# Second layer's first slabs loaded through the last feed-forward part, their differences tied behind it; projections' first weights and one chain placed anew

## The chip, the cores and the metric

The kernel runs on one core of one Trainium2 chip. The metric is device time in microseconds (us): the median of three runs for the kernel as it was, and one further execution that the hardware profiler recorded. All data is float32. The engines are named as in the profile: PE (TensorE; PEld is its weight load), DVE (VectorE), ACT (ScalarE), POOL (GpSimd) and SP (SyncE, which here only issues DMAs).

## The reference

Two layers are computed one after the other on `x` of shape (B, T, F, H) = (4, 512, 128, 64), that is D = F*H = 8192 channels for each of 512 time steps.

```python
# layer 0, per batch b
xn = layernorm(x.reshape(b, t, d), ...)
k, v, r = xn @ Wk, xn @ Wv, sigmoid(xn @ Wr)          # (8192 -> 64 each)
states = scan(s -> decay * s + k * v, over t)
x = x + (r * states @ Wo)                             # 64 -> 8192
xn = layernorm(x);  x = x + gelu(conv over f, 3 taps, 64 -> 64 channels)
xn = layernorm(x);  to = causal conv over t, 3 taps, each channel by itself
x = x + layernorm(to)
x = x + (gelu(x @ W1 + b1) @ W2 + b2)                 # per f: 64 -> 256 -> 64
# layer 1
trend = moving average of x over t, 25 wide
xf = rfft(x - trend, axis=1)[:, :128]                 # 128 modes
ys = einsum('bmnc,cmk->bknc', xf, w_real + 1j * w_imag)
return trend + irfft(ys, n=512)
```

## The kernel before

**Layer 0** (`layer0`, L80) works with channels on the partitions: 8192 channels are 32 pairs (NPR = 32) of 128-channel chunks, each pair a tile of 128 x 2 x 512. For each batch it runs stages: `project` J (loads `xt`, multiplies with the weights `wx`), `scan` Z, `attend_and_convolve` A, `convolve_time` C, `open_feed` O and `feed_forward` F. Each is a Python generator that yields a share of its work; `in_turn` (L835) draws from two of them at a time, so that, for instance, the feed-forward of batch 2 lies between the pieces of the time convolution of batch 3. A generator that yields CHAIN hands over at a place where a chain of small operations runs. The order of matmuls on PE is exactly the order in which the generators are drawn (a manual schedule for that engine). The other engines' instructions are ordered by a planner, by priority; `tc.keep_in_program_order` pins one to its place in the program, and `tc.issue_after(ins)` asks that what is issued inside it comes after `ins`.

The stages draw buffers from pools: `fr` (tiles `xp`, `x1`, `z` and, as a fourth kind, `wx`), `bk` (fetched and intermediate tiles, `kx`, `kh`, `kd`, `k3`, `mid`, `sq`), `const` and others. The last pair of stages is the feed-forward of batch 3 with nothing beside it.

What the change touches in layer 0:

- *The end of a sum over channels.* `add_up` (L252) lets PE add the channels of each tile and its squares into a PSUM bank. `finish` (L256) has ACT copy the bank to `s_sb` (L260) and, after a CHAIN yield, has PE turn it (L264) and DVE copy the means (L269). `moments` (L272) then makes the variance (L275, L276 on DVE), the reciprocal root (L233, L234 on POOL) and the product `mrs` (L278 on DVE). `rows` (L280) spreads each over the partitions (L242 on PE) and copies it out (L286 on ACT), with a CHAIN yield after each. The time convolution ends with `finish` and `moments`; `open_feed`, which begins with `rows`, follows.
- *The first weights of a projection.* For batches 2 and 3, `project` loads weights for the first two pairs (L351), and `scale_weights` (L358) multiplies them in place on DVE, pinned to program order. The matmuls of the projection are at L408. Before it in the same turn lies the end of `attend_and_convolve` of the previous batch, whose last DVE work for a pair is the sum `x2` (L568), stored by POOL (L569).
- *The feed-forward.* Pair i needs the residual: `fetch` (L607) has SP load `kx` and `kh`, DVE computes L692, L693, ACT L701, DVE the sum `x3` (L704). `widen` (L725) is four quarters of eight PE matmuls (L733) with a gelu on ACT each (L738); `narrow` (L740) multiplies back (L746 on PE into `p` and `pb`), and DVE adds the residual (L759) into `x4s`, which for these batches lies in `wx` tiles. `store` (L762), two pairs later, transposes on PE (L765), ACT copies out of PSUM (L773, L778), and POOL stores `ob` to the array `x4` in DRAM (L774).

**Layer 1** (`layer1`, L880) reads `x4` from DRAM. Each batch has 16 slabs of 512 columns. `transform` (L943) goes through them in groups of two; two batches are transformed, then mixed. `shifted_slab` (L934) has SP load one slab with three DMAs (L938, L939, L940; 1.05 MB together) into `xin`, one of five buffers `big` of the pool `io`. ACT copies some edge rows (L956), once for the first and twice for the second slab of a group; DVE makes the difference `v` (L959), the sum `u` (L960) and from that `ev` (L963, two half-size operations a slab). PE multiplies `v` (L971), `ev` (L979) and the edges (L988) with the transform matrices, and ACT copies the banks to `xf` (L995). The inverse tables are loaded by DMAs on ACT's queue (L901). `mix` (L997) and `invert` (L1027) follow. The five buffers are shared by the slabs of the transform, the weights of `mix` and the slabs of `invert`.

Pools are laid out one after the other, and a pool of layer 1 takes the addresses of pools of layer 0 that were given back. The `io` pool thus lies where `fr`, with its `wx` tiles, lay: the first write to it waits for the last reads of what was there.

Of the kernel before, what the change touches and what calls it, by code (L numbers as in the profile page):

```python
# [1 line left out]

# [1 line left out]

# [41 lines left out]
@with_exitstack  # L46
def conv_seq_kernel(
    ctx: ExitStack,
    tc: tile.TileContext,
    x: bass.AP,  # L50
    xt: bass.AP,
    vecs: bass.AP,
    wkvr: bass.AP,
    wo: bass.AP,
    wdec: bass.AP,
    wconv: bass.AP,
    fbias: bass.AP,
    w1: bass.AP,
    fb1: bass.AP,
    w2: bass.AP,  # L60
    fb2: bass.AP,
    wri: bass.AP,
    dftv: bass.AP,
    dftd: bass.AP,
    dfte: bass.AP,
    idfte: bass.AP,
    idfto: bass.AP,
    avg: bass.AP,
    avgh: bass.AP,
    out: bass.AP,  # L70
):
    B = x.shape[0]
    dram = ctx.enter_context(tc.tile_pool(name="dram", bufs=1, space=DRAM))
    x4 = [dram.tile([T, D], F32, tag=f"x4_{b}", name=f"x4_{b}") for b in range(B)]

    layer0(tc, dram, x, xt, vecs, wkvr, wo, wdec, wconv, fbias, w1, fb1, w2, fb2, x4)
    layer1(tc, x4, wri, dftv, dftd, dfte, idfte, idfto, avg, avgh, out)


@with_exitstack  # L80
def layer0(ctx, tc, dram, x, xt, vecs, wkvr, wo, wdec, wconv, fbias, w1, fb1, w2, fb2, x4):
# [10 lines left out]

    decay = ctx.enter_context(tc.tile_pool(name="decay", bufs=1))
    fr = ctx.enter_context(tc.tile_pool(name="fr", bufs=3))
    const = ctx.enter_context(tc.tile_pool(name="const", bufs=1))
    bk = ctx.enter_context(tc.tile_pool(name="bk", bufs=2))
    rowp = ctx.enter_context(tc.tile_pool(name="rowp", bufs=1))
# [49 lines left out]
    nc.vector.tensor_copy(decb, dec.to_broadcast([P, T]))  # L147


    cgr = const.tile([P, NPR, H], F32, name="cgr")  # L150

    at_one = const.tile([P, 2], F32, name="at_one")
    nc.vector.tensor_reduce(at_one[:, 0:1], ident.rearrange("p (q k) -> p q k", k=32)[:, :, 1], mybir.AxisListType.X, ALU.add)
# [142 lines left out]
        return xp  # L296

    def spare(tag, n):
        return fr.tile([P, 2, n], F32, tag=tag, name=tag, bufs={"z": 4, "wx": 2}.get(tag, 3))

    def c_bank():
        return two(ps_c, "c")
# [17 lines left out]
    held = [False]  # L320
    narrowly = set()
    unscanned = [True]


    def project(b):
# [36 lines left out]
        ws, xps, xks = {}, {}, {}  # L362
        if b > 1:
            weights(0)
            for k in range(2):
                scale_weights(k, ws[k], True)
            xps[0] = load_x(b, 0)
        for i in range(NPR):
            first, last = i == 0, i == NPR - 1
# [146 lines left out]
    def attend_and_convolve(b):  # L516
# [29 lines left out]
        def convolve(i):  # L546
            cv = c_bank() if i % 2 or held[0] else two(ps_m, "m")
            for h in range(2):
                for j in range(2):
                    q = 32 * (2 * h + j)  # L550
                    nc.tensor.matmul(
                        cv[h * H : (h + 1) * H, j, :], lhsT=cgr[q : q + 2, i, :], rhs=mb[q : q + 2, :],
                        start=True, stop=False,
                    )
            for j in range(2):
                c = 2 * i + j
                for n, h in neighbours(i % 2, c):
                    if 0 <= n < NCH:
                        rs = halves[rows_of(n // 2 % 2, n - c)]
                        nc.tensor.matmul(  # L560
                            cv[halves[h], j, :], lhsT=ws[n][rs, P:], rhs=zs[n][rs, :], start=False, stop=False
                        )
            for j in range(2):
                c = 2 * i + j
                nc.tensor.matmul(cv[:, j, :], lhsT=ws[c][:, 0:P], rhs=zs[c], start=False, stop=True)
            nc.scalar.activation(cv, cv, AF.Gelu_apprx_tanh)
            x2 = two(bk, "x2")
            nc.vector.tensor_tensor(x2, cv, x1s.pop(i), ALU.add)  # L568
            nc.gpsimd.dma_start(x2d[b][2 * i : 2 * i + 2].rearrange("c p t -> p c t"), x2)  # L569
            sq2 = bk.tile([P, 2, SL], F32, tag="sq", name="sq2")  # L570
            nc.scalar.activation(sq2, x2, AF.Square)  # L571
            for c in (2 * i - 2, 2 * i - 1):
                zs.pop(c, None)
                ws.pop(c, None)
            if i + 2 < NPR:
                scaled(i + 2)
            waiting[i] = x2, sq2
# [26 lines left out]

    def fetch(tag, src, b, i):
        t = bk.tile([P, 2, SL], F32, tag=tag, name=tag, bufs=3 if tag == "kx" else 2)
        nc.sync.dma_start(t, src[b][2 * i : 2 * i + 2].rearrange("c p t -> p c t"))  # L607
        return t


# [36 lines left out]
    def convolve_time(b):  # L647
# [34 lines left out]
            yield 7.0 * (NPR + 2) / (n + 2)  # L682
        mean, sq = yield from finish(st, bank, 4)
        causal[b] = moments(mean, sq, 4)


    def residual(b, i):
# [27 lines left out]
    def feed_forward(b):  # L715
# [12 lines left out]
        def widen(i, q):  # L728
            x3 = x3s[i]
            pm = unit()  # L730
            for h in range(2):
                for j in range(2):
                    nc.tensor.matmul(  # L733
                        pm[halves[j], h, :], lhsT=w1_sb[halves[h], q * H : (q + 1) * H], rhs=x3[halves[h], j, :],
                        start=True, stop=True,
                    )
            mid = mids[i, q] = bk.tile([P, 2, SL], F32, tag="mid", name="mid", bufs=4)
            nc.scalar.activation(mid, pm, AF.Gelu_apprx_tanh, bias=fb1_sb[:, q : q + 1])  # L738

        def narrow(i, q):  # L740
            if q == 0:
                sums2[i] = of_p(), ps_s.tile([P, SL], F32, tag="s", name="pb")
            mid = mids.pop((i, q))
            for h in range(2):
                for j in range(2):
                    nc.tensor.matmul(  # L746
                        sums2[i][j][halves[h], :], lhsT=w2_sb[halves[j], q, :], rhs=mid[halves[j], h, :],
                        start=q == 0, stop=q == 3,
                    )
            if q < 3:  # L750
                return
            x3 = x3s.pop(i)
            if lag > 1:
                pair = spare("wx", 4 * S + SL)[:, :, 0:SL]
                x4s[i] = [pair[:, j, :] for j in range(2)]
            else:
                x4s[i] = [bk.tile([P, SL], F32, tag="x4t", name="x4t", bufs=3) for _ in range(2)]
            for j, pa in enumerate(sums2.pop(i)):
                nc.vector.scalar_tensor_tensor(x4s[i][j], pa, fb2_sb, x3[:, j, :], ALU.add, ALU.add)  # L759

        def store(i):
            pt = unit()  # L762
# [22 lines left out]
        for i in range(NPR + lag):  # L785
            if i >= lag:
                store(i - lag)
            for q in range(4):
                done += quarter
                if i < NPR:  # L790
                    if q < 2:
                        widen(i, q + 2)
                    elif i + 1 < NPR:
                        widen(i + 1, q - 2)
                    if i + 2 < NPR and q == 1:
                        coming = residual(b, i + 2)
                    if i + 2 < NPR and q == 3:
                        x3s[i + 2] = add_residual(b, i + 2, *coming)
                    narrow(i, q)
# [62 lines left out]
    with tc.manual_schedule(engines={nc.tensor.engine}):  # L862
        for _ in project(0):
# [10 lines left out]
            ((2, (O, 0.05), (F, 0.95)), (3, (C, 0.95), (O, 0.05))),  # L874
            ((3, (F, 1.0)), (3, (nothing, 1.0))),
        )


@with_exitstack
def layer1(ctx, tc, x4, wri, dftv, dftd, dfte, idfte, idfto, avg, avgh, out):  # L880

# [7 lines left out]
    G = 2  # L891

    dft = ctx.enter_context(tc.tile_pool(name="dft", bufs=1))
    io = ctx.enter_context(tc.tile_pool(name="io", bufs=2))
    const = ctx.enter_context(tc.tile_pool(name="const1", bufs=1))
    spec = ctx.enter_context(tc.tile_pool(name="spec", bufs=1))
# [29 lines left out]
            nc.vector.tensor_copy(dst, src)  # L926

    def slab(b, s):
        xin = io.tile([P, NT, SL], F32, tag="big", name="xin", bufs=5)
        nc.sync.dma_start(  # L930
            xin, x4[b][:, s * SL : (s + 1) * SL].rearrange("(c p) d -> p c d", p=P)
        )
        return xin

    def shifted_slab(b, s):
        xin = io.tile([P, NT, SL], F32, tag="big", name="xin", bufs=5)
        c = slice(s * SL, (s + 1) * SL)
        nc.sync.dma_start(xin[TURN:P, 0, :], x4[b][0 : P - TURN, c])  # L938
        nc.sync.dma_start(xin[0:TURN, 0, :], x4[b][T - TURN : T, c])  # L939
        nc.sync.dma_start(xin[:, 1:NT, :], x4[b][P - TURN : T - TURN, c].rearrange("(c p) d -> p c d", p=P))  # L940
        return xin

    def transform(b, xf):  # L943

        for g in range(NS // 2):
            edge = io.tile([P, SL], F32, tag="edge", name="edge")
            uv, ev, pf = [], [], []
            for k in range(2):
                s = 2 * g + k
                c = slice(s * SL, (s + 1) * SL)  # L950
                xin = shifted_slab(b, s)
                ends = xin[0 : 2 * TURN, 0, :]
                if k == 0:
                    first = ends
                for q in (32,) if k == 0 else (H, H + 32):
                    nc.scalar.copy(edge[q : q + 2 * TURN, :], ends)  # L956
                u = io.tile([P, 2, SL], F32, tag="uv0", name="u")
                v = io.tile([P, 2, SL], F32, tag="uv1", name="v")
                nc.vector.tensor_tensor(v, xin[:, 0:2, :], xin[:, 2:4, :], ALU.subtract)  # L959
                nc.vector.tensor_tensor(u, xin[:, 0:2, :], xin[:, 2:4, :], ALU.add)  # L960
                t = io.tile([P, 2, SL], F32, tag="ev", name="ev")
                for i, op in enumerate((ALU.add, ALU.subtract)):
# [34 lines left out]
    def mix(xf):  # L997

        xc = xf.rearrange("p b r (a c l) -> p b r a c l", c=H, l=2)
        for g in range(H // CG):  # L1000

            w = io.tile([P, CG, 2, 2, M], F32, tag="big", name="w", bufs=5)
            nc.sync.dma_start(w, wri[:, g * CG : (g + 1) * CG, :, :, :])
            w4 = w[:, :, 1, 0, :].rearrange("p c (n i m) -> p c n i m", n=2, i=2)[:, :, :, 0, :]
            for t in (w4, w[:, :, 1, 1, 0:H]):
# [23 lines left out]
    def invert(b, xf):  # L1029
# [3 lines left out]
        def waves(s):  # L1033
# [12 lines left out]
            for i, op in enumerate((ALU.add, ALU.subtract)):  # L1046
                nc.vector.tensor_tensor(even[:, i, :], ev[0], two, op)
            for i in range(2):
                pm = io.tile([P, 2, SL], F32, tag=f"uv{i}", name="pm")
                for k, op in enumerate((ALU.add, ALU.subtract)):  # L1050
                    nc.vector.tensor_tensor(pm[:, k, :], even[:, i, :], od[i], op)
                halves[s].append(pm)
# [1 line left out]
        def trends(s):  # L1054
            c = slice(s * SL, (s + 1) * SL)
            xin = slab(b, s)
            halo = io.tile([P, SL], F32, tag="edge", name="halo")
            for j in range(NT):
                at = 32 * j
                if j > 0:  # L1060
# [137 lines left out]
```

## Time and profile before

| what | us |
|---|---|
| median of three runs | 3730.86 |
| lowest and highest | 3727.31, 3736.47 |
| the profiled execution's own time | 3727.17 |
| its span, first to last instruction | 3725.4 |
| PE busy | 3519.4 |
| DVE busy | 2671.6 |
| ACT busy | 1779.8 |
| POOL busy | 450.4 |
| granted PE clock, mean share of full | 0.983 |

A row of the groups or the timeline gives line, engine and operation, then output and input tiles with their shapes. In the timeline the first number is the start from the span's begin, the second the duration, and the bracket at the end how long the engine had stood idle and what released it. A row of the list of waits gives who waited for whom, the total, how often, and the longest. Matmuls overlap in PE's pipeline, and their ends are modelled; a busy PE is not a PE at its peak.

### The profile page before, as it was taken

Reading aid. Unit: us, or ns where it says so; the run is one execution under the profiler, and the core shown is the slowest. Engines: PE = TensorE matmul, PEld = TensorE weight load, DVE = VectorE, ACT = ScalarE, POOL = GpSimd, SP = SyncE. Lnnn points to the kernel's source line nnn. Section 1 sums busy time; section 2 is a strip of 40 time slices with the busy share of each in tenths; the row PEclk is TensorE's granted clock in tenths of the full one; section 3 lists DMA queues with packets and bytes.
Section 4 is the critical chain, followed back from the end, with each engine's and each line's share of the span. In section 5 each row is a group of like instructions: output and inputs, shape, how many; then the busy total and the mean of one; then the engine's idle time right before and its main releaser. Section 6 shows DMA issues by size and latency. Waiting matters only on the chain. (4 is left out here: it accounts for less than half of the span.)

```text
span 3725.4 us, 53006 instructions
## 1 busy us (share of the span) xinstructions
PE 3519.4 (94%) x20041; PEld 1366.8 (37%) x20041; DVE 2671.6 (72%) x3498; ACT 1779.8 (48%) x2331; POOL 450.4 (12%) x654
## 2 busy tenths in 40 slices
PE   9999999989999999999999989899989999899998
PEld 4433322224333223433322333333323843328433
DVE  4455569976777896677789699946658277792677
ACT  0013346546666565566656588878855200152100
POOL 0000012220011211001122122100000000001000
PEclk9999999999999999999999999999999999999999
DMA  9867647777885787788478677645569479994687
GB/s 313 282 211 243 227 154 270 254 264 259 293 295 176 249 275 267 265 292 296 167 240 286 210 245 268 233 154 194 199 202 285 154 231 295 300 295 167 214 286 263
DMA packets 427223, 910.29 MB, mean 244 GB/s; under 512 B 32728, under 2 KB 83160, under 8 KB 422872
## 3 DMA queue, kind: packets, MB, share of 16 engines
q1 hardware_dynamic: 353136, 636.92, 52.7%
q0 software_dynamic: 71680, 268.46, 19.8%
q8 instruction: 160, 2.62, 0.3%
q10 hardware_dynamic: 2152, 1.51, 0.1%
q14 instruction: 95, 0.78, 0.1%
HBM read 638.26 MB, written 268.50 MB: 243 GB/s over the span
## 5 line engine op out<-in xcount | busy, mean ns | idle before, releaser
L746 PE MATMUL p<-mid,w_sb 64*64 64x512 f32 x2048 | 560.8, 595 | 24.0 <-DVE wx L759 23.3
L746 PE MATMUL pb<-mid,w_sb 64*64 64x512 f32 x2048 | 533.4, 595 | 0.0
L738 ACT ACTIVATE mid<-c,fb_sb 128x1024 f32<-128x1024 f32 x256 | 284.6, 1112 | 94.5 <-PE c L733 92.3
L738 ACT ACTIVATE mid<-m,fb_sb 128x1024 f32<-128x1024 f32 x256 | 285.0, 1113 | 91.2 <-PE m L733 89.7
L733 PE MATMUL c<-x,w_sb 64*64 64x512 f32 x2016 | 281.6, 606 | 11.1 <-ACT mid L738 7.0
L733 PE MATMUL m<-x,w_sb 64*64 64x512 f32 x2016 | 283.3, 609 | 5.6 <-ACT ob L778 3.4
L746 PEld LDWEIGHTS p<-mid,w_sb 64*64 64x64 f32 x2048 | 160.4, 134 | 289.6 <-issue 244.0
L408 PE MATMUL a<-xp,wx 128*128 128x512 f32 x512 | 240.0, 613 | 6.6 <-issue 6.6
L1044 ACT COPY two<-a 128x512 f32<-128x512 f32 x64 | 37.5, 587 | 428.4 <-PE a L1039 428.4
L1067 PE MATMUL b<-xin,avg_sb 128*128 128x512 f32 x512 | 230.8, 593 | 3.3 <-DVE xin L1073 3.3
L1073 DVE TENSOR_TENSOR xin<-b,pm 128x512 f32<-128x512 f32 x256 | 159.1, 684 | 99.2 <-PE b L1070 84.3
L571 ACT ACTIVATE sq<-x 128x1024 f32<-128x1024 f32 x128 | 135.2, 1056 | 181.4 <-DVE x L568 181.3
L626 DVE SCALAR_TENSOR_TENSOR to<-kd,vec,to 128x510 f32<-128x510 f32 (+1 forms) x272 | 197.7, 747 | 10.5 <-ACT to L622 9.4
L701 ACT ACTIVATE kd<-kd,vec 128x512 f32<-128x512 f32 x256 | 193.1, 805 | 3.3 <-DVE kd L693 3.3
L252 PE MATMUL st<-x,ones 128*32 128x512 f32 x512 | 174.2, 611 | 10.7 <-DVE x L568 10.6
L926 DVE COPY xf<-b 128x256 f32<-128x256 f32 x128 | 54.4, 425 | 178.9 <-PE b L1013 170.0
L626 DVE SCALAR_TENSOR_TENSOR z<-x,vec,z 128x511 f32<-128x511 f32 x240 | 176.2, 747 | 5.0 <-ACT z L622 3.6
L704 DVE TENSOR_TENSOR x<-kd,kx 128x1024 f32<-128x1024 f32 x126 | 154.2, 1224 | 33.8 <-ACT kd L701 33.8
L532 DVE TENSOR_TENSOR x<-a,xp 128x1024 f32<-128x1024 f32 x128 | 156.3, 1221 | 29.8 <-PE a L530 27.3
L530 PE MATMUL a<-rst,wo_sb 64*128 64x512 f32 x512 | 148.6, 654 | 27.4 <-DVE x L532 25.4
L759 DVE SCALAR_TENSOR_TENSOR x4t<-p,fb_sb,x 128x512 f32<-128x512 f32 x64 | 47.8, 747 | 159.8 <-PE pb L746 157.4
L569 POOL DMA_DIRECT2D x<-x x128 | 93.5, 731 | 566.7 <-DVE x L568 561.7
(269 smaller groups left out, 6830.1 us busy)
## 6 DMA issues: line engine op xcount, KB each, us to landing
xp<-in_xt SPq DMA_DIRECT2D x256, 512.0 KB
kh<-to SPq DMA_DIRECT2D x156, 512.0 KB
x<-x POOLq DMA_DIRECT2D x128, 512.0 KB, 4.6
kx<-x SPq DMA_DIRECT2D x128, 512.0 KB
x<-ob POOLq DMA_DIRECT2D x64, 1024.0 KB, 8.1
xin<-x SPq DMA_DIRECT2D x64, 1024.0 KB
out<-xin POOLq DMA_DIRECT2D x64, 1024.0 KB, 5.9
x<-x SPq DMA_DIRECT2D x96, 512.0 KB
```

The lines of the kernel that those rows point to most:

```text
L252: nc.tensor.matmul(st[32 * q : 32 * q + 32, :], lhsT=ones, rhs=src[:, j, :], start=first, stop=last,)
L408: nc.tensor.matmul(pa[:, k, :], lhsT=wq[:, j, k * P : (k + 1) * P], rhs=xp[:, j, :], start=first and j == 0, stop=last and j == 1,)
L530: nc.tensor.matmul(at[:, j, :], lhsT=wo_sb[js, :], rhs=rst[js, :], start=True, stop=True)
L532: nc.vector.tensor_tensor(x1, at, xp, ALU.add)
L626: tap = nc.vector.scalar_tensor_tensor(to[:, j, k:], xr[:, j, : SL - k], vec[:, w, c], to[:, j, k:], ALU.mult, ALU.add)
L701: tc.keep_in_program_order(nc.scalar.activation(d[:, j, :], d[:, j, :], AF.Identity, bias=vec[:, B4, c], scale=vec[:, G4, c]))
L704: nc.vector.tensor_tensor(x3, d, x2, ALU.add)
L733: nc.tensor.matmul(pm[halves[j], h, :], lhsT=w1_sb[halves[h], q * H : (q + 1) * H], rhs=x3[halves[h], j, :], start=True, stop=True,)
L738: nc.scalar.activation(mid, pm, AF.Gelu_apprx_tanh, bias=fb1_sb[:, q : q + 1])
L746: nc.tensor.matmul(sums2[i][j][halves[h], :], lhsT=w2_sb[halves[j], q, :], rhs=mid[halves[j], h, :], start=q == 0, stop=q == 3,)
L1067: nc.tensor.matmul(po[j], lhsT=avg_sb[:, j, :], rhs=xin[:, j, :], start=True, stop=False)
L1073: nc.vector.tensor_tensor(by_n(xin[:, j, :]), by_n(po[j]), by_c(pm[j % 2][:, j // 2, :]), ALU.add)
```

## The change

It has four parts. First, layer 1 gets a pool `slabs` of its own for the five `big` buffers, the edge rows and the differences `v`, placed ahead of `io`, where layer 0's `decay` and `fr` lay; layer 0 moves `wx` out of `fr` into a new pool `wxp`, and the tile `cgr` from `const` into `fr`. Second, the loads of slabs 0 to 4 of batch 0 are issued after fetches of the feed-forward of batch 3 (pairs 12, 16, 20, 24 and 28 are then being fetched), their edge copies after the last gelu of pair 29, and the first two `v` after the last residual sum of pair 29. Third, the time convolution of batch 3 yields CHAIN once more at its end, after `moments`. Fourth, for batches 2 and 3 the first weights' scalings are no longer pinned in program order but tied behind the sum `x2` of pair 30 of the batch before.

In the order that results, PE's instructions differ in one place alone: between L264 of the time convolution of batch 3 and its first spread L242 there now stand the transposes of one pair and three units of the feed-forward of batch 2 (L733 and L746), and three fewer stand after it. On SP the fifteen slab DMAs stand between the fetches, three after every fourth pair. On ACT five edge copies stand between two gelus of pairs 29 and 30, and the sixth one gelu later. On DVE two `v` stand before the residual sums of pair 30, and the scalings stand before the last L568 of the batch before. POOL's order is the same.

```diff
@@ layer0
     fr = ctx.enter_context(tc.tile_pool(name="fr", bufs=3))
+    wxp = ctx.enter_context(tc.tile_pool(name="wxp", bufs=2))
...
-    cgr = const.tile([P, NPR, H], F32, name="cgr")
+    cgr = fr.tile([P, NPR, H], F32, name="cgr", bufs=1)
...
     def spare(tag, n):
-        return fr.tile([P, 2, n], F32, tag=tag, name=tag, bufs={"z": 4, "wx": 2}.get(tag, 3))
+        if tag == "wx":
+            return wxp.tile([P, 2, n], F32, tag=tag, name=tag)
+        return fr.tile([P, 2, n], F32, tag=tag, name=tag, bufs=4 if tag == "z" else 3)
...
+    last_fetch = [None]
+    after = {"sync": []}
@@ project
         if b > 1:
             weights(0)
-            for k in range(2):
-                scale_weights(k, ws[k], True)
+            with tc.issue_after(begin[project]):
+                for k in range(2):
+                    scale_weights(k, ws[k])
@@ attend_and_convolve
-            nc.vector.tensor_tensor(x2, cv, x1s.pop(i), ALU.add)
+            whole_x2 = nc.vector.tensor_tensor(x2, cv, x1s.pop(i), ALU.add)
+            if i == NPR - 2:
+                begin[project] = whole_x2.ins
@@ fetch
-        nc.sync.dma_start(t, src[b][2 * i : 2 * i + 2].rearrange("c p t -> p c t"))
+        last_fetch[0] = nc.sync.dma_start(t, src[b][2 * i : 2 * i + 2].rearrange("c p t -> p c t"))
@@ convolve_time
         causal[b] = moments(mean, sq, 4)
+        if b == B - 1:
+            yield CHAIN
@@ feed_forward, widen
+            gelu = nc.scalar.activation(mid, pm, AF.Gelu_apprx_tanh, bias=fb1_sb[:, q : q + 1])
+            if i == NPR - 3:
+                after["scalar"] = gelu.ins
@@ feed_forward, narrow
+                summed = nc.vector.scalar_tensor_tensor(x4s[i][j], pa, fb2_sb, x3[:, j, :], ALU.add, ALU.add)
+            if i == NPR - 3:
+                after["vector"] = summed.ins
@@ feed_forward
                         coming = residual(b, i + 2)
+                        if b == B - 1 and i % 4 == 2:
+                            after["sync"].append(last_fetch[0].ins)
@@ layer1
+    slabs = ctx.enter_context(tc.tile_pool(name="slabs", bufs=2))
     io = ctx.enter_context(tc.tile_pool(name="io", bufs=2))
...
+    def behind(b, s, ins):
+        return tc.issue_after(ins) if b == 0 and s < 5 else nullcontext()
@@ transform
-                xin = shifted_slab(b, s)
+                with behind(b, s, after["sync"][min(s, 4) + 2]):
+                    xin = shifted_slab(b, s)
...
-                    nc.scalar.copy(edge[q : q + 2 * TURN, :], ends)
+                with behind(b, s, after["scalar"]):
+                    for q in (32,) if k == 0 else (H, H + 32):
+                        nc.scalar.copy(edge[q : q + 2 * TURN, :], ends)
...
-                v = io.tile([P, 2, SL], F32, tag="uv1", name="v")
-                nc.vector.tensor_tensor(v, xin[:, 0:2, :], xin[:, 2:4, :], ALU.subtract)
+                v = slabs.tile([P, 2, SL], F32, tag="uv1", name="v")
+                with behind(b, s, after["vector"]):
+                    nc.vector.tensor_tensor(v, xin[:, 0:2, :], xin[:, 2:4, :], ALU.subtract)
```

## The prediction

> **What bounds the kernel now.** I read the page first: engines, then the costliest groups. The first line says that TensorE (PE) is the bound nearly throughout.
>
> ```profile
> PE 3519.4 (94%) x20041; PEld 1366.8 (37%) x20041; DVE 2671.6 (72%) x3498; ACT 1779.8 (48%) x2331; POOL 450.4 (12%) x654
> ```
>
> The change takes no matmul away, so it can win only among the 3725.4 - 3519.4 = 206 us in which PE stands. PE's list of waits says whose they are (total, count, longest):
>
> ```profile
> PE a L971 <- DVE v L959: 20.4, 12, 9.4
> PE a L242 <- POOL rs L234: 12.3, 6, 4.0
> PE a L408 <- issue: 6.6, 2, 4.1
> ```
>
> Row one is the second layer's transform, waiting for the slabs' differences `v`. Row two holds the wait for the moments' reciprocal root, row three the projections of batches 2 and 3 (two waits in all). The timelines of PE, DVE, SP and ACT around these places then give the sizes. The largest, between the layers (start, duration, engine, line, what, idle before):
>
> ```profile
> 2742.55 1.31 PE L765 MATMUL c<-ident,wx 128*128 128x128 f32 x8
> 2753.26 3.37 PE L971 MATMUL a<-v,dftd_sb 128*64 128x512 f32 x8 [9.40 <-DVE v L959]
> 2758.30 1.94 PE L971 MATMUL a<-v,dftd_sb 128*64 128x512 f32 x8 [1.68 <-DVE v L959]
> ```
>
> ```profile
> 2744.01 0.34 SPq L938 DMA_DIRECT2D xin<-x  x1
> ```
>
> ```profile
> 2751.93 1.22 DVE L959 TENSOR_TENSOR v<-xin 128x1024 f32<-128x1024 f32 x1 [8.78 <-DMA xin<-x]
> 2834.25 2.50 DVE L963 TENSOR_TENSOR ev<-u 128x512 f32<-128x512 f32 x4
> 2841.20 2.50 DVE L963 TENSOR_TENSOR ev<-u 128x512 f32<-128x512 f32 x4
> ```
>
> PE's last transposes (L765) end at 2743.86, only then does SP issue slab 0 (2744.01), it lands at 2751.9, and PE starts at 2753.26. Later a group of two slabs takes 6.95 us (from 2834.25 to 2841.20), which is DVE's work: two `v` and two `u` of 1.13 each, four half-size `ev`, 2.4. PE needs 3.65 + 1.9 + 1.1 = 6.65. So late in the transform DVE is the bound and PE waits 0.4 a group.
>
> **Part 1: slabs 0 to 4 early.** *Removed*: the release wait and the landing of slab 0. *Added to the feed-forward of batch 3 (2482 to 2744)*: 15 DMAs on SP, three a slab, one slab per four pairs behind a fetch of L607; six edge copies on ACT; two `v` on DVE.
>
> The DMAs: 1.05 MB a slab beside a stage whose window from 2500 to 2700 us shows DMA engines 0.56 busy. At the 3.5 us a slab of the late transform this is 17.5 us of transfer in 262 us. The slab stands in SP's queue ahead of the next pair's fetches and can delay them by its 3.5. Their lead covers it: the last `kh` is issued at 2698.95 and first read by L692 at 2714.00, 15 us later. Without this cover each slab would cost up to 3.5. I take 0 (ends 0 and 5 in all). POOL's stores are untouched.
>
> The edge copies are not free. They sit on ACT behind a gelu (L738) of pair 29, ahead of the next gelu:
>
> ```profile
> 2723.06 1.11 ACT L738 ACTIVATE mid<-c,fb_sb 128x1024 f32<-128x1024 f32 x1 [0.25 <-PE c L733]
> 2724.78 1.11 ACT L738 ACTIVATE mid<-m,fb_sb 128x1024 f32<-128x1024 f32 x1 [0.60 <-PE m L733]
> ```
>
> ACT idles 0.6 per 1.72 us unit there. Five copies of 0.635 (three took 1.90 at 2757.46) are 3.2; less the 0.6, a gelu, and the narrowing matmuls that need it, come 2.5 late. PE is full, so I book 2.4 (ends 1 and 4): its end goes to 2746.3. The two `v` fit in DVE's idle of 5 us a pair: nothing.
>
> Then PE needs only the last PSUM copy (L773), at about 2747.4. DVE does sixteen groups of 6.95 less the two `v`: 111.2 - 2.3 = 108.9 from 2746.3, so to 2855.2; PE's tail behind the last `ev` is 3.1 (before: 2872.7 to 2875.8). That is 2858.3 against 2875.8. Slab 5 can't be issued before group 0's edge matmuls have read slab 0's buffer (2747.4 + 6.65 = 2754) and lands some 7 later, while DVE wants it at about 2759: 2 to 4 us of stall. End 2861.5: **gain 14.3**.
>
> Two rates speak for less. The Trainium skill's page "DMA: Bandwidth & Descriptors", section Specifications, gives a core about 358 GB/s from HBM: 27 slabs of 1.05 MB would take 79 us, no bound at all. The rows say otherwise: in the window 2820 to 2840 the engines moved 293 GB/s at 0.97 busy, so 27 slabs cost 97 us of the 104 from 2754 to the end. I use the row: DMA barely keeps up, and at 3.7 us a slab (the early spacing, 2769.01 to 2772.70) the end is 2754 + 7 + 26 x 3.7 + 6.5 = 2864: gain 12. Low end 8 (ACT: its loads of the inverse tables, L901, wait for the last store to land, issued about 2748 in the new kernel, and the `xf` copies that free PSUM queue behind them; wanted at 2761, margin 1 to 3 us, cost if missed up to 4). High end 18.
>
> **Part 2: one chain placed anew.** At the end of the time convolution of batch 3, PE does L264 and then waits for DVE and POOL:
>
> ```profile
> 2451.67 1.05 PE L264 MATMUL a<-pick,s_sb 128*128 128x2 f32 x8
> 2456.76 2.08 PE L242 MATMUL a<-ident,rs 128*128 128x128 f32 x8 [4.04 <-POOL rs L234]
> 2458.63 1.92 PE L765 MATMUL m<-ident,wx 128*128 128x128 f32 x8
> ...
> 2465.11 1.16 PE L242 MATMUL a<-ident,mrs 128*128 128x128 f32 x8
> ```
>
> With the extra yield, transposes and three units of feed-forward (some 8 us) stand between L264 and L242: 4.04 goes. After it the same kinds of instruction took 2.08, 1.92 and 1.99 instead of about 1.1 (the granted clock is 0.50 from 2456 to 2462): 3 more. Late next: L242, and so the first residuals, come some 3 us later against the rest; DVE's last `x4s` adds (L759) of the old batch queue behind L692, L693 and L704 of the new one, and the transposes L765 behind them wait until about 2474: a new wait of some 2 to 4 us. **Gain 4.5**, ends 1 and 8.
>
> **Part 3: first weights of a projection.** On DVE, eight (batch 2) or six (batch 3) scalings L358 stood behind `mrs`, which waits for POOL:
>
> ```profile
> 802.46 0.16 DVE L278 TENSOR_TENSOR mrs<-me,rs 128x4 f32<-128x4 f32 x1 [2.43 <-POOL rs L234]
> 802.54 1.92 DVE L358 TENSOR_SCALAR wx<-wx,vec 128x192 f32<-128x192 f32 x8
> ```
>
> ```profile
> 802.96 3.75 PE L408 MATMUL a<-xp,wx 128*128 128x512 f32 x4 [4.05 <-issue]
> 1461.23 7.72 PE L408 MATMUL a<-xp,wx 128*128 128x512 f32 x12 [2.58 <-issue]
> 1469.60 5.40 PE L408 MATMUL a<-xp,wx 128*128 128x512 f32 x12
> ```
>
> They move ahead of the last `x2` add (L568). In batch 3 that add follows 3.72 us of DVE idle, which takes 1.46 whole: the 2.58 go. In batch 2 DVE is busy, the add comes 1.9 later and PE's wait for it (1.80) grows to about 3.6: of 4.05, some 2.2 remain.
>
> The clock: after the 2.58 gap twelve matmuls took 7.72, the next twelve 5.40. The skill's page "TensorE: Matmul & The Clock Gate", Part 1, lets the clock drop only after an idle window of about 3.4 us. By it, a gap of 2.58 costs no clock and batch 3 is worth 2.6; by the row (granted clock 0.69 from 1461 to 1469) it is 2.6 + 2.3 = 4.9. I take the row, less 0.9 for a gap that stays between L264 and its neighbours: **4** (2 to 5). Batch 2: 2.2 plus 1.9 of slow clock (four at 3.75 against 1.85): **4** (-1 to 6, as the longer wait ahead can itself slow the clock).
>
> Moving `wx` to its own pool and `cgr` into the released one changes addresses alone: 0.
>
> **Sum.** 14.3 + 4.5 + 4 + 4 = 26.8. The profiled execution took 3727.17 (span 3725.4), 3.7 under the median of 3730.86; 3727.2 - 26.8 = 3700.4, or on the median's basis 3704.
>
> **Rivals.**
> *Pace hides the start (22%).* The slabs' transfer at 3.7 or the PSUM copies behind L901 set the transform's end, and the new wait of part 2 eats its gain: 8 + 1 + 5 = 14, 3717. For it: DMA engines 0.92 to 1.06 busy over the whole transform. Against: groups of 6.95 late in it, so transfer can keep DVE's pace.
> *The slabs wait anyway (4%).* If a slab's issue still depended on the old pool, nothing of part 1 is left but its 2.4: gain 10, 3721. Against: what its three DMAs overwrite was last read early in the batch.
> *Slower (6%).* The 15 DMAs stand in SP's one queue among the fetches that feed pairs 12 to 31. If a slab delays a fetch beyond its lead, PE starves once a slab. It decides from 26.8 / 5 = 5.4 us a slab; at two transfers late (7 us) plus a slow clock after the gap (3 us) it costs 50: 3754. For it: SP's issue is in order. Against: 0.56 busy DMA.
>
> **How the numbers follow.** Full gain 68%, 3704, own range 3695 to 3712; the rivals 22, 4 and 6. 0.3% (11.2 us) is what a measurement here can tell from no change, so faster means under 3719.7. The first case and four fifths of the second are faster, 0.86; same 0.08; slower 0.06. The range goes from the high ends (18 + 8 + 5 + 3 = 34, with spread 3691) to the pace rival, 3718.
>
> **What would show it.** PE's gap before the first L971 falls from 9.4 to 1 or 4 us and the transform lasts 111 to 117 us instead of 122.5; no PE wait in the feed-forward of batch 3 beyond about 2.4 us near its end; L242 <- POOL rs without its 4.0; L408 <- issue without 4.1 and 2.6. Wrong, if L733 or L746 wait for fetches from pair 12 on, if L971 waits repeatedly for `xf` or `xin`, or if the mix that follows gives the lead back.

## The result, and the profile after

The changed kernel took 3704.85 us in the median of five runs (3697.14 to 3714.69). The kernel before took 3727.31 over the five runs it had by then (3720.68 to 3736.47). The ratio is 0.9935 with an interval of 0.9913 to 0.9957, that is 24 us faster (16 to 32). The prediction said 3704 with a range of 3691 to 3718. A second measurement on another occasion gave 0.9926 (0.991 to 0.9941).

The profiled execution took 3708.95 (span 3707.2), only 18.2 us less span than before. Both kernels issue the same 20041 matmuls, in the same order but for the few at the end of the last time convolution. So I compare the start of the n-th matmul in both traces; the growth of that lead over a stretch is what the stretch gained.

| stretch | predicted | changed kernel | its second recording |
|---|---|---|---|
| up to the end of the attention of batch 1 (nothing changed there) | 0 | -8.6 | -3.4 |
| start of batch 2's projection | 4 | 4.3 | 3.4 |
| start of batch 3's projection | 4 | 2.9 | 2.6 |
| end of batch 3's time convolution | 4.5 | 4.9 | 5.0 |
| last feed-forward, its end | -2.4 | -3.7 | -3.6 |
| gap between the layers | 8.3 | 8.2 | 8.2 |
| transform (122.55 before) | 8.4 | 8.5 | 5.8 |

For the two rows of the gap and the transform I split the prediction's own times: start of the transform 2747.4, end 2861.5. The first row is not the change: it is how far two executions of the same instructions lay apart in their first 780 us, and it hides a third of the gain in this one execution. The changed places sum to 25.1 us in one recording and 21.4 in the other; the stretches between them, which are not in the table, add 1.7 and 3.1.

Line numbers have moved: L759 is now L771, L765 is L779, L242 and L264 are L243 and L265, L408 is L414, L568 is L574, L252 is L253, L733 is L743, L738 is L748, L773 is L787, L956 is L980, L959 is L984, L963 is L988, L971 is L996. The page's first line, and PE's list of waits:

```profile
PE 3520.8 (95%) x20041; PEld 1358.2 (37%) x20041; DVE 2669.1 (72%) x3498; ACT 1778.5 (48%) x2331; POOL 449.0 (12%) x654
```

```profile
PE a L996 <- DVE v L984: 13.0, 14, 3.7
PE a L243 <- POOL rs L235: 8.2, 5, 3.4
PE c L779 <- DVE wx L771: 3.4, 1, 3.4
```

PE is as busy as before (3520.8 against 3519.4) in a shorter span. The wait for `v` fell from 20.4 to 13.0 and its longest part of 9.4 is gone; the waits of the projections for "issue" have left the list; a new row of one wait of 3.4 is the price of the moved chain. PE's timeline between the layers, and ACT's where the edge copies now stand:

```profile
2723.05 1.09 PE L779 MATMUL m<-ident,wx 128*128 128x128 f32 x8 [1.32 <-ACT mid L748]
2724.82 1.99 PE L743 MATMUL c<-x,w_sb 64*64 64x512 f32 x8 [0.69 <-ACT mid L748]
...
2740.73 1.31 PE L779 MATMUL c<-ident,wx 128*128 128x128 f32 x8
...
2743.20 3.65 PE L996 MATMUL a<-v,dftd_sb 128*64 128x512 f32 x16 [1.16 <-ACT ob L787]
```

```profile
2717.56 1.11 ACT L748 ACTIVATE mid<-c,fb_sb 128x1024 f32<-128x1024 f32 x1 [0.25 <-PE c L743]
2718.70 3.15 ACT L980 COPY edge<-xin 32x512 f32<-32x512 f32 x5
2721.88 1.11 ACT L748 ACTIVATE mid<-m,fb_sb 128x1024 f32<-128x1024 f32 x1
```

The transform starts 1.16 us after the last transposes, released by the last PSUM copy (L787), no longer by a landing. Ahead of it five edge copies in a row hold the next gelu back, and PE pays 1.32 + 0.69 of idle time; then a unit runs at 1.99 instead of 1.04.

The end of the time convolution:

```profile
2451.06 1.05 PE L265 MATMUL a<-pick,s_sb 128*128 128x2 f32 x8
...
2458.28 1.16 PE L243 MATMUL a<-ident,rs 128*128 128x128 f32 x8
...
2473.03 1.97 PE L779 MATMUL c<-ident,wx 128*128 128x128 f32 x8 [3.42 <-DVE wx L771]
```

L243 no longer waits. The last transposes of the old batch wait 3.42 instead, for sums (L771) that on DVE stand behind the first residuals of the new batch.

The projections of batch 2 (first two lines) and batch 3:

```profile
802.73 1.67 PE L253 MATMUL st<-x,ones 128*32 128x512 f32 x2 [3.82 <-DVE x L574]
808.25 1.98 PE L414 MATMUL a<-xp,wx 128*128 128x512 f32 x4 [0.26 <-DVE me L270]
...
1461.43 7.11 PE L414 MATMUL a<-xp,wx 128*128 128x512 f32 x12 [0.26 <-DVE me L270]
1469.19 5.40 PE L414 MATMUL a<-xp,wx 128*128 128x512 f32 x12
```

Both gaps before L414 are 0.26. In batch 2 the wait for the last `x2` grew from 1.80 to 3.82. In batch 3 the first twelve matmuls still take 7.11, though the gap ahead of them is gone.

### The profile page after: what moved, and what is told of

It is laid out like the page before. It is cut to its first block, busy times and chain, and to the rows that moved or that the text cites. A ratio compares the mean times of both kernels' runs of the same rounds, so it can differ in the third digit from the quotient of the medians.

```text
span 3707.2 us, 52993 instructions
## 1 busy us (share of the span) xinstructions
PE 3520.8 (95%) x20041; PEld 1358.2 (37%) x20041; DVE 2669.1 (72%) x3498; ACT 1778.5 (48%) x2331; POOL 449.0 (12%) x654
## 5 line engine op out<-in xcount | busy, mean ns | idle before, releaser
L758 PE MATMUL p<-mid,w_sb 64*64 64x512 f32 x2048 | 553.1, 597 | 17.5 <-DVE wx L771 17.5
L748 ACT ACTIVATE mid<-m,fb_sb 128x1024 f32<-128x1024 f32 x256 | 284.9, 1113 | 92.2 <-PE m L743 90.9
L748 ACT ACTIVATE mid<-c,fb_sb 128x1024 f32<-128x1024 f32 x256 | 284.5, 1111 | 92.2 <-PE c L743 90.0
L743 PE MATMUL c<-x,w_sb 64*64 64x512 f32 x2016 | 280.6, 609 | 13.9 <-ACT mid L748 7.6
L743 PE MATMUL m<-x,w_sb 64*64 64x512 f32 x2016 | 282.6, 612 | 7.4 <-ACT ob L792 5.3
L414 PE MATMUL a<-xp,wx 128*128 128x512 f32 x512 | 237.4, 608 | 0.5 <-DVE me L270 0.5
L253 PE MATMUL st<-x,ones 128*32 128x512 f32 x512 | 175.6, 610 | 14.0 <-DVE x L574 14.0
L771 DVE SCALAR_TENSOR_TENSOR x4t<-p,fb_sb,x 128x512 f32<-128x512 f32 x64 | 47.8, 746 | 159.5 <-PE pb L758 157.1
```

The source lines that it names most:

```text
L253: nc.tensor.matmul(st[32 * q : 32 * q + 32, :], lhsT=ones, rhs=src[:, j, :], start=first, stop=last,)
L414: nc.tensor.matmul(pa[:, k, :], lhsT=wq[:, j, k * P : (k + 1) * P], rhs=xp[:, j, :], start=first and j == 0, stop=last and j == 1,)
L743: nc.tensor.matmul(pm[halves[j], h, :], lhsT=w1_sb[halves[h], q * H : (q + 1) * H], rhs=x3[halves[h], j, :], start=True, stop=True,)
L748: gelu = nc.scalar.activation(mid, pm, AF.Gelu_apprx_tanh, bias=fb1_sb[:, q : q + 1])
L758: nc.tensor.matmul(sums2[i][j][halves[h], :], lhsT=w2_sb[halves[j], q, :], rhs=mid[halves[j], h, :], start=q == 0, stop=q == 3,)
```

## The experiments

In the runs below, a lead is that of the n-th matmul as in the table above.

**Each part alone.** The slabs' part, in the changed kernel, without the other two:

```diff
-        if b == B - 1:
-            yield CHAIN
-            with tc.issue_after(begin[project]):
-                for k in range(2):
-                    scale_weights(k, ws[k])
+            for k in range(2):
+                scale_weights(k, ws[k], True)
```

> The slabs' part alone: the chain of the last time convolution and the scalings stay as before. My theory (the parts add, each acts in its own place): PE's gap before the first L996 is 1 to 1.5 us as in the changed kernel, the lead over the kernel before grows by 12 to 14 us between the middle of the last feed-forward and the end of the transform and nowhere else, so 3714 against 3727, ratio 0.9965. Rival (most of the gain comes from the two layer 0 edits and the pace of the transform eats the early start): under 8 us, ratio over 0.998.

Measured: ratio 0.9964 (0.995 to 0.9979), 13 us. The lead grew by 13.1 from the middle of the last feed-forward to the end of the transform: -3.7 at the feed-forward's end, +8.2 in the gap, +8.7 in the transform (113.9 us). My theory stood, the rival fell.

The further yield alone, in the kernel before:

```diff
         causal[b] = moments(mean, sq, 4)
+        if b == B - 1:
+            yield CHAIN
```

> The one further CHAIN yield alone. My theory: PE's wait of 4.0 us before the spread of rs (L242) goes, a wait of about 3.4 us stands before the last transposes of the old batch (L765, behind DVE L759), and slow clock follows that new gap instead of the old one; the lead at the start of the last feed-forward is 4 to 5 us, ratio 0.9988. Rival (the new wait takes the place of the old one in full): 0 to 1 us, ratio 1.000.

Measured: ratio 0.9987 (0.9973 to 1.0001); the interval touches 1, so the whole time doesn't settle it. The place does: the lead grows by 5.1 there, with the same new wait of 3.42. The new wait takes back half, not all.

The scalings alone, in the kernel before (`begin[project]` is set at the sum `x2` of pair 30):

```diff
-            for k in range(2):
-                scale_weights(k, ws[k], True)
+            with tc.issue_after(begin[project]):
+                for k in range(2):
+                    scale_weights(k, ws[k])
```

> The scalings of the first weights alone, tied behind the sum x2 of pair 30. My theory: batch 2 gains 4 us (gap before L408 from 4.05 to 0.3, wait before the channel sums of the last pair from 1.8 to 3.8), batch 3 gains 3 us, together 7, ratio 0.998. On the clock in batch 3: if the slow clock follows the gap of 2.58 us, the first twelve L408 take 5.4 us once the gap is gone; if it follows the small matmuls and waits around L264, they still take about 7.

Measured: ratio 0.9989 (0.9972 to 1.0006), again not settled by the whole time. At the places: 4.1 in batch 2, of which 1.3 is given back within 20 us, where a block of slow clock follows (from 808.8, 6.83 long), and 2.9 in batch 3. The first twelve matmuls of batch 3 take 7.1, so the slow clock doesn't follow the gap of 2.58. The three ratios multiply to 0.9940, against 0.9935 and 0.9926 for all together: as far as these intervals tell, the parts add.

**What sets the pace of the transform.** First without the loads: only the first five slabs of batch 0 and of batch 2 are loaded, and for all others, those of batches 1 and 3 too, the transform works on what the five buffers hold.

```diff
-                    xin = shifted_slab(b, s)
+                    xin = shifted_slab(b, s) if b % 2 == 0 and s < 5 else kept[-5]
+                kept.append(xin)
```

> The changed kernel with the slab loads left out after the first five of batches 0 and 2: the transform then works on slabs that were loaded before, so part of its input is wrong. It tells whether DVE or the transfer sets the pace. My theory (DVE, 6.95 us a group): first L996 to the last copy of the first transform takes 110 to 112 us instead of 114, with PE still waiting 0.4 us a group for v. Rival (the transfer paces it): PE becomes the bound at 6.65 us a group and the transform takes under 108.5 us.

Measured: 111.2 us for the transform. DVE is busy without a break (20.00 of 20 us in four windows), and PE waits for it a little in most groups:

```profile
PE b L999 <- DVE v L987: 2.8, 7, 0.4
PE a L999 <- DVE v L987: 2.4, 6, 0.4
```

So 111.2 is DVE's floor, and the loads cost 2.9 us of the 114.1. (The lead grew again by 5.3 us in the second transform, whose slabs after the fifth are missing too; that is no part of the question.)

Then with less work on DVE, and the loads in place: the second of the two `ev` operations is left out, and its matmuls read the first one's result.

```diff
-                for i, op in enumerate((ALU.add, ALU.subtract)):
-                    nc.vector.tensor_tensor(t[:, i, :], u[:, 0, :], u[:, 1, :], op)
+                nc.vector.tensor_tensor(t[:, 0, :], u[:, 0, :], u[:, 1, :], ALU.add)
...
-    pf[k][r][q : q + H // 2, :], lhsT=dftv_sb[:, i, r, :], rhs=ev[k][:, i, :],
+    pf[k][r][q : q + H // 2, :], lhsT=dftv_sb[:, i, r, :], rhs=ev[k][:, 0, :],
```

> The changed kernel with the second of the two ev operations left out (its matmuls read the first one's result, so the output is partly wrong). DVE needs 5.8 us a group then, PE 6.65. My theory (DVE sets the pace, the transfer is just behind it): the transform takes 109 to 112 us instead of 114. If DVE alone set it and the transfer had room: 106 to 108. If the transfer sets it: 113 to 115, unchanged.

Measured: 113.7, as good as unchanged. DVE's waits for slabs before `u` within the transform, in this kernel and then in the changed one:

```profile
DVE u L985 <- DMA xin<-x: 13.9, 12, 1.7
```

```profile
DVE u L985 <- DMA xin<-x: 1.4, 2, 1.3
```

Windows of this kernel's trace (busy times, then granted clock, DMA share, GB/s):

```profile
core 0: us, PE busy (x) PEld busy (x) DVE busy (x) ACT busy (x) POOL busy (x), PEclk, DMA share, GB/s
...
2763.00:2783.00 20.00, 17.86 (x124) 5.51 (x128) 16.13 (x17) 11.85 (x21) 0.00 (x0) 1.00 1.00 283
2783.00:2803.00 20.00, 18.29 (x136) 5.32 (x128) 17.71 (x18) 11.57 (x20) 0.00 (x0) 1.00 1.02 298
2803.00:2823.00 20.00, 18.17 (x140) 5.39 (x140) 16.00 (x17) 10.63 (x19) 0.00 (x0) 1.00 1.00 291
```

DVE now stands 2 to 4 us in each 20 and waits for slabs, while the DMA engines are busy all the time at 283 to 298 GB/s. My theory (DVE sets the pace) fell: with five slabs in hand the transfer ends the transform, and DVE's floor lies 2.9 us below it. SP issues most slabs only when DVE's `v` has freed a buffer (11 such waits, 42.3 us in the changed kernel's transform); that more buffers would not help is argued from the busy DMA engines and was not run. The seven recordings with early loads and all of DVE's work have transforms of 113.9 to 116.8 us, all above the floor (122.55 to 125.4 in three without early loads). Transfers that vary fit this spread: in the second recording of the changed kernel, 116.8 long, `u` waited 4.6 us for slabs instead of 1.4. It was not tested apart.

**The price of the edge copies.** Each of the six behind a gelu of its own:

```diff
-                with behind(b, s, after["scalar"]):
-                    for q in (32,) if k == 0 else (H, H + 32):
+                for q in (32,) if k == 0 else (H, H + 32):
+                    with behind(b, s, after["scalar"][min(64 + 12 * s + (q == H + 32) * 4, 127)]):
                         nc.scalar.copy(edge[q : q + 2 * TURN, :], ends)
```

Here `after["scalar"]` is the list of all gelus of that feed-forward, four a pair.

> The changed kernel with the six early edge copies spread over the last feed-forward, each behind a gelu of its own (pairs 16 to 26) instead of five together behind one. My theory (the 3.7 us that the last feed-forward lost against the kernel before come from five copies of 0.63 in a row on ACT, and the slow clock of PE after them): the loss falls to 0 to 0.6 us, the gap before the first L996 and the transform stay at 1.4 and 114. Rival (the loss comes from elsewhere, the slabs' transfers or the early differences on DVE): the loss stays over 3 us.

Measured: the loss at the feed-forward's end fell from 3.7 to 0.3; gap (1.16) and transform (114.7) stayed. A copy now fills the 0.6 us that ACT has free in a unit:

```profile
2590.64 1.11 ACT L749 ACTIVATE mid<-m,fb_sb 128x1024 f32<-128x1024 f32 x1 [0.60 <-PE m L744]
2591.78 0.62 ACT L981 COPY edge<-xin 32x512 f32<-32x512 f32 x1
```

Without a tie, left to the planner:

```diff
-                with behind(b, s, after["scalar"]):
-                    for q in (32,) if k == 0 else (H, H + 32):
-                        nc.scalar.copy(edge[q : q + 2 * TURN, :], ends)
+                for q in (32,) if k == 0 else (H, H + 32):
+                    nc.scalar.copy(edge[q : q + 2 * TURN, :], ends)
```

> The changed kernel with the edge copies not tied to any gelu: the planner sets them where it expects the slabs to land, one, two, one and two together, from pair 14 on. My theory: three single or double copies cost PE at most 0 to 0.7 us each, under 1.5 us in all, instead of 3.7; a copy that stands ahead of its slab's landing would hold ACT and PE, and then it costs more than 3.7.

Measured: the last feed-forward lost 40.7 us, and the one execution that was timed took 3742.75, against 3715.78 for the kernel before beside it. The planner set each copy where it thought the slab had landed, and ACT then stood before it for 9 us, with the gelus queued behind. ACT's and PE's waits in that stretch, and one copy:

```profile
ACT edge L979 <- DMA xin<-x: 35.0, 4, 9.0
```

```profile
PE m L779 <- ACT mid L748: 31.3, 4, 8.0
```

```profile
2543.47 0.62 ACT L979 COPY edge<-xin 32x512 f32<-32x512 f32 x1 [8.78 <-DMA xin<-x]
```

Of my two expectations the second came true. ACT's four waits make 31.3 us of waiting on PE; with each comes a block of slow clock (6.83 or 10.24 us long), and half of the matmul time in these four blocks, 9.8 us, is the rest of the 40.7. Tying the copies behind a late gelu is worth ten times what it costs.

**The slabs among the fetches.** All five early slabs behind the first of the five fetches:

```diff
-                with behind(b, s, after["sync"][min(s, 4) + 2]):
+                with behind(b, s, after["sync"][2]):
```

> The changed kernel with all five early slabs behind the first of the five fetches instead of one per four pairs. My theory (a slab delays the next fetches by its 3.5 us, and their lead of about 15 us less a landing of 6 covers two, not five): PE waits once in the middle of the last feed-forward, 5 to 12 us with its slow clock. Rival (the transfers share the engines and delay nothing): 0.

Measured: the five slabs are issued within 19 us (2531.4 to 2550.3), with one pair of fetches between the DMAs of the fourth, and PE has no wait at all from it. PE's list of waits in the last feed-forward has the same two rows as the changed kernel, 1.3 and 0.7, both from the edge copies, and the lead doesn't move until those. The DMA share was 0.92 to 1.06 in the 30 us from 2530 and back at 0.69 in the 20 us from 2560. The rival was right: within this lead five slabs delay nothing that PE feels.

**A version that does better in places.** The spread copies, and the scalings behind the last `x2`:

```diff
-            if i == NPR - 2:
+            if i == NPR - 1:
                 begin[project] = whole_x2.ins
```

> The changed kernel with two edits: the early edge copies spread as before, each behind a gelu of its own, and the scalings tied behind the sum x2 of the last pair (31) instead of pair 30. My theory: the spread saves 3.3 us again; the scalings no longer hold up the last x2 of batch 2, so PE's wait before the last channel sums falls from 3.8 to about 1.8 and the gap before the projection stays at 0.3 in both batches, 1.5 to 2.5 us more in batch 2, 0 in batch 3. In all 5 us under the changed kernel, ratio to the kernel before 0.992. Rival (the scalings behind the last x2 delay the means and with them the projection's start or the sums after it): no gain or a loss in batch 2.

> The changed kernel itself once more, on the same chip as the run beside it: ratio to the kernel before 0.9935 by the first measurement, 0.9945 by the sum of the parts' own runs (0.9964, 0.9987 and 0.9989 multiplied give 0.9940).

Measured together: 0.9923 (0.9906 to 0.994) for the version, 0.9926 (0.991 to 0.9941) for the changed kernel again. By the whole time no difference is shown. By place, the spread saves its 3.3 again, and batch 2 starts with 6.7 instead of 3.4 of lead (the wait for `x2` is back at 1.8 and the gap stays 0.3). In batch 3 nothing comes of it: its first twelve matmuls take 5.42 for 7.11, and then PE waits for the next thing on DVE.

```profile
1459.73 5.42 PE L415 MATMUL a<-xp,wx 128*128 128x512 f32 x12 [0.26 <-DVE me L270]
...
1481.84 1.09 PE L744 MATMUL m<-x,w_sb 64*64 64x512 f32 x8 [2.00 <-DVE x L715]
```

In the changed kernel's second recording that wait is 0.28: what the clock gave was returned 20 us later. (Whether the edit gave it is not shown, see the last section.) Where nothing differs, between 900 and 1400 us, the version lost 4.1 us and the changed kernel gained 3.4, which takes up the rest.

## Why the prediction was right

**The sum.** 26.8 predicted, 21.4 to 25.1 measured by place, 24 by the runs. The time 3704 is met partly by luck: the median of before, on which it stood, fell by 3.5 as runs were added. In the sum of high ends behind the range, batch 2 enters with 3, where its own text has 6; with 6 the range would have begun at 3688.

**Part 1, 14.3 predicted, 13.0 and 10.4 in the changed kernel's recordings, 13.1 alone.** The gap came out as worked (1.16 of idle before the first product; 1.1 predicted), and so did the transform's length (114.1 and 114.1). The edge copies were under-sized: 2.4 booked, 3.7 paid. The term that was missing is the clock: the idle time was 2.0, and one block of half clock (the trace records it from 2724.7, 3.41 long) added 1.7. The spread version shows both gone together. DVE's sixteen groups of 6.95 were right as a floor: 2747.4 to 2858.3 is 110.9 us, and 111.2 was measured without loads. They failed as the bound: the transfer is the bound, which the prediction had as the rate that "barely keeps up", and put at 12 us of gain. The stall of 2 to 4 us for slab 5 that it added on top has the right size (2.9), but neither the place nor the reason, and that is luck. Slab 5 did not wait for PE's edge matmuls. SP issued it at 2744.56, as soon as DVE's first two `u` had ended at 2744.5 (in the code, PE reads nothing of the second slab of a group but its edge copies, so its buffer is free then); the issue that followed PE's edge matmuls, at 2749.76, was the next slab's. DVE's row of 2784.22 holds its first stall for a slab in the transform, 40 us in; in the windows from 2752 to 2852 it stood 2.4 us in all.

```profile
2744.56 0.32 SPq L956 DMA_DIRECT2D xin<-x  x1
...
2749.76 0.30 SPq L956 DMA_DIRECT2D xin<-x  x1
```

```profile
2742.14 2.36 DVE L985 TENSOR_TENSOR u<-xin 128x1024 f32<-128x1024 f32 x2 [0.80 <-PE c L779]
...
2784.22 1.22 DVE L985 TENSOR_TENSOR u<-xin 128x1024 f32<-128x1024 f32 x1 [1.25 <-DMA xin<-x]
```

The price of the loads in the feed-forward, 0, was right, with more room than the argument gave it: not two but five transfers fit.

**Part 2, 4.5 predicted, 4.9 measured.** The wait of 4.04 went, the new wait predicted at 2 to 4 measured 3.42. But the clock term was wrong in its place: the 3 us of slow matmuls were not saved, they moved behind the new wait (1.97, 1.99, 1.93 at 2473 to 2478). In their stead the wait of 2.35 for L759 that stood in the profile before went as well, which the prediction had not counted. PE's idle time there fell from 6.7 (4.04, 2.35 and 0.3 in short gaps) to 3.4, that is by 3.3; where the last 1.6 comes from I can't show. So the 4.9 is near the 4.5 in part by luck: two errors, the clock and the second wait, nearly cancel.

**Part 3.** Batch 2: predicted 4, measured 3.2 to 4.3 over eight recordings with this edit, and in three of them 1.3 of it was given back within 20 us. The wait for `x2` was put at 3.6 and is 3.8; the gap went; the slow four matmuls went from 3.75 to 1.98. Batch 3: predicted 4, measured 2.9 (2.6 once). The mis-sized term is again the clock. By the Trainium skill's page "TensorE: Matmul & The Clock Gate", Part 1, the clock falls back after an idle window of some 3.4 us; that would have given 2.6, and the row 4.9. Neither names the cause, and the traces do not bear the rule out as a limit on one gap. The granted clock in the windows around it, before, then changed, then with the scalings behind the last sum:

```profile
1461.00:1469.00 8.00, 7.77 (x15) 3.53 (x15) 1.28 (x6) 0.00 (x0) 0.00 (x0) 0.69 0.61 183
```

```profile
1461.00:1469.00 8.00, 7.74 (x21) 3.66 (x20) 0.65 (x4) 0.59 (x1) 1.26 (x2) 0.79 0.90 315
```

```profile
1463.00:1471.00 8.00, 8.00 (x25) 3.96 (x25) 2.31 (x8) 0.00 (x0) 1.26 (x2) 1.00 0.95 307
```

With PE's idle gaps down to 0.72 and 0.26 around the eight small matmuls of L265, one block of half clock still follows in the changed kernel, and none follows in the last one, with the same two gaps. So the gap of 2.58 added its own length and 0.6 of slow clock, not 2.3.

**The rivals.** That the pace hides the start was half right: the transfer sets the pace, but it costs 2.9 of the 17 that gap and transform gained together. That the slabs wait anyway, and that they starve the feed-forward, didn't happen. The price that could really have turned the change into a loss is one that the prediction didn't have: an edge copy placed ahead of its slab's landing, 40.7 us.

## What to carry to other kernels

A load moved early under a busy stage was free here even in a burst; what it drags with it on an in-order engine was not: five short copies behind one gelu cost 3.7 us, one behind each of six gelus 0.3, and copies left where a planner guessed the landing 40.7. Before a gain is booked to an engine's pace, take that engine's work away in thought and ask what the next limit is: DVE's floor and the transfer's lay 3 us apart, and only the second counted. And an idle gap's slow clock should be booked apart from the gap, as something that may move to the next gap or be given back at the next wait.

## What the runs showed of the hardware

The granted clock in these traces falls to one half in blocks of 3.41 us or multiples of it (but for one of 7.0 to 9.9 us at the very end of each trace). 3.41 us at half clock cost at most 1.7 us of matmul work, and that is the whole difference between 7.11 and 5.40 for the same twelve matmuls. Blocks appeared after idle gaps much shorter than a block: after 1.32 + 0.69 us in the feed-forward, and around L265 after 0.72 + 0.26.

Within each trace the blocks start and end (the last end apart) on one grid of 3.413 us, to within 0.003 us: in the changed kernel, 1461.78 and 2724.71 lie 370 steps apart. In all eight recordings with the scalings tied behind pair 30, the 0.72, the eight small matmuls of L265 (1.05) and the 0.26, together 2.03 us, fall into one step of that grid, and the next step is a block. In the version with the scalings behind the last sum, a line of the grid (1459.54) divides the same 2.03 us into 1.85 and 0.18, and no block follows. So where the stretch fell on the grid may have decided, and not the edit. That is one execution against eight, and how much idle time in a step it takes is not shown.

Executions of the same instructions differed by up to 16 us (leads from -8.6 to +7.2) in their first 780 us, where no edit was made.
